# Filling the rotary attention's ring buffers inside layer 0, and running one batch's feed-forward inside the rotary attention's opening

## The chip, the cores and the metric

The kernel runs on one core of a Trainium2 chip. That core has five engines with a queue of instructions each, taken in order: TensorE (matrix products, PE in the profile; PEld is its weight loads), VectorE (DVE), ScalarE (ACT), GpSimd (POOL) and SyncE (SP, which here only issues DMAs). Products land in PSUM, everything else lies in SBUF; both are cut into 128 partitions. The metric is the device time of the whole program in microseconds (us), the median of several runs.

## The reference

Four layers of a network in float32, on 4 batches of 1024 tokens with 128 channels. Around the change it computes this:

```
x = x + 0.5 * _L0_ffn_ref(_layernorm(x), ...)      # experts, second time in layer 0
x = x + 0.5 * _L1_ffn_ref(_layernorm(x), ...)      # gated feed-forward
x = x + _L1_attn_ref(_layernorm(x), ...)           # rotary attention, 16 heads of 8
x = x + 0.5 * _L1_ffn_ref(_layernorm(x), ...)
...
def _L1_ffn_ref(x, w_gate, w_up, w_down):
    gate = x @ wg.T ; up = x @ wu.T                # 128 -> 384
    return (silu(gate) * up) @ wd.T
```

The rotary attention turns queries and keys by position, takes the softmax of their products over all 1024 keys, and weighs the values with it. Nothing in any of these steps crosses from one batch to another.

## The kernel before

The residual `X[b]` of each of the four batches stays in SBUF, channels in the partitions, tokens along the row (128x1024, two halves of 512).

**Layer 0** (`layer0`, `macaron`) is written as lanes of tasks. `lanes` interleaves them by costs written into their `yield`s; that gives the order of the program text. The order on each engine is then set at compile time by a list scheduler with a model of the hardware, which may issue an instruction of a later stage early when its operands and its memory are free. The lanes are: the expert blocks (`experts`: POOL gathers token rows by indirect DMA, L452, and scatters results, L478), the combines (`combine`: two `c_y` loads on SP, scaling, four transposes and one add into `X[b]` for each half, L503 to L513), and a lane with the routes, the layer's own attention (`middle0` to `middle3`, `l0_attn`) and then the feed-forward of each batch, `last(0)` to `last(3)` (`l1_ffn`, L604 to L637). `last(b)` waits for `combine1{b}`; `last(3)` takes PSUM banks from the pool `main`, the others from `side`. Attention and feed-forward hold their SBUF pools `l0a` and `l1f0` on the right side of the memory until layer 0 ends.

**The rotary attention** (`l1_attn`) has its TensorE order written by hand (`manual_schedule`): its own matrix products keep the order of the text, while those of other stages may still come in between. It first clears its rings on POOL (L663 to L669): four `qz`, four `kz`, four `va` (128x1024 each) and two `top`. Heads lie eight channels to a group of 32 partitions; row 0 of each group of `kz` is set to one, group by group, as `va`'s first column is. All of them lie in the pool `l1a`, which waits for the pools that held its memory before as a whole. Then `prepare(0)` normalizes batch 0 and makes dense queries, keys and values: a centering product (`cen`), variances (`var`), a broadcast of 1/std (`bc`), four projections, of which cosine and sine halves are multiplied on DVE (`rot1`, `rot2`) and added on POOL (`qd`, `kd`, L709), and a value product (`vp`). `spread(n)` copies a group of heads into a ring by eight small DMAs on SP and a POOL copy into `va`.

The main loop then takes 256 units. In each unit `greatest` finds row maxima (products of 32 rows, reduced on DVE, L736), and `scores` and `values` work 11 units (`LEAD`) behind it, so in the first 11 units only `greatest` runs. `prepare` of the next batch is spread over the units from the eleventh on. The products use PSUM pools of two double banks (`l1m`, tag `two`), three banks (`l1s`, tag `s`) and one (`l1o`).

```
            for z in (*qz, *kz, *va, *tops):
                nc.gpsimd.memset(z, 0.0)
            for z in va:
                nc.gpsimd.memset(z[:, :, :, 0:1], 1.0)
            for z in kz:
                for g in range(4):
                    nc.gpsimd.memset(z[32 * g : 32 * g + 1, :], 1.0)
```

Layer 2 then takes its SBUF pools from the right side again (`l2d`, `l1f1`, `l2a`).

Of the kernel before, what the change touches and what calls it, by code (L numbers as in the profile page):

```python
# [13 lines left out]
AF = mybir.ActivationFunctionType  # L14
ALU = mybir.AluOpType
AX = mybir.AxisListType

P = 128
# [3 lines left out]
NT = S // P  # L22
# [5 lines left out]
BLOCKS = blocks_of(GT)  # L28
MOE_W = 2 * FC * P + FC + D
HIDC = 3  # L30
LN_EPS = 1e-5
GN_EPS = 1e-5 * 64
L2_EPS = 1e-6
# [27 lines left out]
def _constants():  # L61

    p = np.arange(P)
    f = np.float32
    n8, n16 = np.arange(8), np.arange(16)
    t = np.arange(P)

    c0 = [
        ("ident", np.eye(P, dtype=f)),
        ("mean", np.full((P, P), 1.0 / P, f)),  # L70
        ("rev", np.broadcast_to((8 - n8).astype(f), (P, 8))),
        ("below", (p[:, None] < p[None, :]).astype(f)),
        ("ones", np.ones((P, P), f)),
        ("lane", np.broadcast_to(p.astype(f), (P, P))),
        ("column", np.broadcast_to(np.arange(BLOCKS, dtype=f), (P, BLOCKS))),
        ("full", np.broadcast_to((SLOTS * np.arange(GT)).astype(f), (P, GT))),
        ("center", np.eye(P, dtype=f) - f(1.0 / P)),
        ("place", 1.0 + p[:, None].astype(f)),
        ("tile", np.broadcast_to(np.arange(2 * GT, dtype=f), (P, 2 * GT))),
        *[  # L80
            (f"spare{g}", (1.0 + 2 * g * NT * P + p[:, None] + P * np.arange(blocks_of(g * NT))).astype(f))
            for g in range(1, GROUP + 1)
        ],
    ]

    dd = p % HD
    freqs = np.power(f(10000.0), -np.arange(0, HD, 2, dtype=f) / f(HD)).astype(f)
    angles = (np.arange(S, dtype=f)[:, None] * freqs).astype(f)
    sin, cos = np.sin(angles).astype(f), np.cos(angles).astype(f)
    sign = np.where(dd < HD // 2, -1.0, 1.0).astype(f)  # L90
    c1 = [
        ("cos", cos.T[dd // 2]),
        ("sin", sin.T[dd // 2] * sign[:, None]),
    ]

    n = np.maximum(t[None, :] - p[:, None], 0)
    bits = ((n[:, None, :] >> np.arange(7)[:, None]) & 1).astype(f)
    c2 = [("bit", bits), ("nobit", 1 - bits), ("causal", (t[None, :] >= p[:, None]).astype(f))]

    h, turned = p // HD, np.arange(2)[None, :, None]  # L100
    c3 = [
        ("sums", (h[:, None, None] == np.arange(32) - NH * turned).astype(f)),
        ("vrows", ((p % 32)[:, None, None] == NH * turned + h).astype(f)),
        ("bonus", (h[:, None] == p % NH).astype(f)),
        ("gcenter", np.eye(P, dtype=f) - (p[:, None] % NH == p % NH).astype(f) / HD),
        ("gmean", (p[:, None] % NH == n16).astype(f) / HD),
    ]
    return {"c0": c0, "c1": c1, "c2": c2, "c3": c3}
# [99 lines left out]
class Macaron:  # L208
# [433 lines left out]

    def l1_attn(self, m, c1):
        nc = self.nc
        scale = HD ** -0.5
        LEAD, RING = 11, 4
        v = nc.vector
        PE = mybir.EngineType.PE  # L650
        with ExitStack() as ctx:
            enter = ctx.enter_context
            wp = enter(self.tc.tile_pool(name="l1a", bufs=2))
            p1 = enter(self.psum("l1m", 2))
            p2 = enter(self.psum("l1s", 3))
            pa = enter(self.psum("l1o", 1))
            enter(self.tc.manual_schedule(engines={PE}))
            two = lambda shape=(P, S): self.t(p1, list(shape), "two")
            ring = lambda tag, shape, n: [self.t(wp, shape, f"{tag}{i}", bufs=1) for i in range(n)]
            qz, kz = ring("qz", [P, S], RING), ring("kz", [P, S], RING)  # L660
            va = ring("va", [P, NT, 4, 32], RING)
            tops = ring("top", [P, 4, 4, 32], 2)
            for z in (*qz, *kz, *va, *tops):  # L663
                nc.gpsimd.memset(z, 0.0)
            for z in va:
                nc.gpsimd.memset(z[:, :, :, 0:1], 1.0)
            for z in kz:
                for g in range(4):
                    nc.gpsimd.memset(z[32 * g : 32 * g + 1, :], 1.0)  # L669
            ons, dense = {}, {}  # L670

            def project(w, x):
# [134 lines left out]
                    v.scalar_tensor_tensor(X[:, c], y, m["bo"], X[:, c], ALU.add, ALU.add)  # L807
                    yield

            for _ in prepare(0):  # L810
                pass
            for n in range(RING):
                spread(n)
            units = B * 4 * 16
# [1 line left out]
            for k in range(units + LEAD + 1):  # L816
                first = k if k < units else None
                second = k - LEAD if 0 <= k - LEAD < units else None
                if k % 16 == LEAD + 1 and RING <= k // 16 + RING - 1 < 4 * B:
                    spread(k // 16 + RING - 1)  # L820
                if k % 64 == 10 and k // 64 + 1 < B:
                    running.append(prepare(k // 64 + 1))
                if first is not None and first % 8 == 0:
                    nms[first // 8] = self.t(wp, [P, 4, 2, 4], "nm", bufs=3)
                    qms[first // 8] = self.t(wp, [P, HALF], "qm", bufs=3)
                es = {}
                for pair in range(2):
                    if first is not None:
                        greatest(first, pair, nms[first // 8])
                    if second is not None:  # L830
                        scores(second, 1 - pair, qms[second // 8], es)
                    if pending:
                        at, then = pending
                        if at % 8 == 0 and pair == 0:
                            o = self.t(pa, [P, HALF], "o")
                        values(at, o, then, pair)
                if pending and at % 8 == 7:
                    running.append(normalized(at // 8, o))
                pending = (second, es) if second is not None else None
                if first is not None and first % 8 == 7:  # L840
                    running.append(shifted(first // 8, nms[first // 8], qms[first // 8]))
                running = [r for r in running if next(r, self) is not self]
            while running:
                running = [r for r in running if next(r, self) is not self]

# [402 lines left out]

    def layer0(self, moe, m, right, enter, ffn):
        m["wqkvc"] = self.centered(m["wqkv"], 3 * D)  # L1250
        pa, pf = enter(right, "l0a"), enter(right, "l1f0")
        side, main = self.side, self.main

        def more(route):
            attn = lambda b, *after: (f"middle{b}", after, lambda: self.l0_attn(side, pa, m, b))
            last = lambda b, ps: (f"last{b}", (f"combine1{b}",), ffn(pf, ps, b))
            return (
                [
                    route(0, (0,), ps=main), route(0, (1,)), route(0, (2, 3)),
                    *[attn(b, f"combine0{b}") for b in range(B)],  # L1260
                    last(0, side), last(1, side), last(2, side), last(3, main),
                ],
                [route(1, (0, 1), "middle0", "middle1", "combine03"), route(1, (2,), "middle2"), route(1, (3,), "middle3")],
            )


        groups = [(0,), (1,), (2, 3)], [(0, 1), (2,), (3,)]
        marks = {(0, (0,)): "_1", (0, (1,)): "_2", (0, (2, 3)): "_0", (1, (0, 1)): "_0", (1, (2,)): "_1", (1, (3,)): "_2"}
        self.macaron("l0", moe, AF.Gelu, groups, marks, more)
# [29 lines left out]

    def run(self, stages):  # L1300
        nc = self.nc
        self.X = []
        self.c0 = self.load("c0")
        for b in range(B):
            X = self.t(self.res, [P, S], f"x{b}")
# [20 lines left out]
        for n, name in enumerate(stages):  # L1326
# [3 lines left out]
            if name in ("l0", "l2"):  # L1330
                with self.psum("main", 4) as self.main, self.psum("side", 4) as self.side, sb(name + "moe") as self.fp:
# [2 lines left out]
                    nc.vector.tensor_copy(moe["both"][:, 0:P], self.c0["center"])  # L1334
                    nc.scalar.copy(moe["both"][:, P:], self.centered(moe["rw"], NE))
                    with ExitStack() as right:
                        enter = lambda stack, name, bufs=2: stack.enter_context(sb(name, bufs, side="right"))
                        m = dict(weights(name + "a"))
                        ffn = lambda wp, ps, b: lambda: self.l1_ffn(ps, wp, weights("l1f"), b)
                        if name == "l2":  # L1340
                            self.c2 = weights("c2")
                        if name == "l0":
                            self.layer0(moe, m, right, enter, ffn)
                        else:
                            self.layer2(moe, m, right, enter, ffn)
            elif name == "l1_attn":
                with sb("ln1") as self.lnp:
                    self.l1_attn(weights("l1a"), weights("c1"))
            else:
                f, t, c3 = self.l3_ffn_weights(weights("l3f")), self.l3_time_weights(weights("l3a")), weights("c3")  # L1350
                self.layer3(f, t, c3)
        for b in range(B):
            nc.sync.dma_start(out=self.out[:, b * S : (b + 1) * S], in_=self.X[b])

# [35 lines left out]
```

## Time and profile before

| what | us |
|---|---|
| median of 3 runs | 3132.94 (3131.44 to 3135.03) |
| the profiled execution's own time | 3239.76 |
| span of its trace, first to last instruction | 3237.5 |
| TensorE busy in the span | 2766.3 (85%) |
| VectorE busy | 1834.3 (57%) |
| ScalarE busy | 1626.5 (50%) |
| GpSimd busy | 799.3 (25%) |
| layer 0's last expert product ends | 887.0 |
| last batch's feed-forward, first to last product | 897.8 to 928.1 |
| first product of `greatest` | 965.8 |
| first product of `scores` | 1008.6 |
| last product of `values` | 2024.4 |

Durations are taken from the one profiled execution, which took 107 us longer than the median of the undisturbed runs. In the lists below, a line gives start, duration, engine, source line, operation, output and inputs by the program's names with their shapes, how many instructions are merged into the line, and in brackets how long the engine stood idle before it and what released it. `PEclk` is the share of TensorE's full clock that was granted.

### The profile page before, as it was taken

The page shows a single profiled execution, that of the slowest core. Times are in us where ns is not written, and L with a number is a line of the kernel's source. Part 1 is how long each engine was busy: PE and PEld are TensorE (multiplying, and loading weights), DVE is VectorE, ACT ScalarE, POOL GpSimd, SP SyncE. Part 2 cuts the span into 40 slices and gives each one's busy share as a digit, 9 for nine tenths or more (in the row PEclk, how much of TensorE's full clock was granted, in tenths as well). Part 3 has the DMA queues.
Part 4 walks back from the last instruction along what each step waited for, and adds up shares of the span by engine and source line. Part 5 has one row for each costly group of instructions (what it writes and reads, how often), then busy time and mean ns, then how long its engine had stood idle before and what let it go on. Part 6 is the DMA issues. An engine that isn't in the chain of part 4 may idle for free. (4 is left out here: it accounts for less than half of the span.)

```text
span 3237.5 us, 47507 instructions
## 1 busy us (share of the span) xinstructions
PE 2766.3 (85%) x17694; PEld 1584.7 (49%) x17694; DVE 1834.3 (57%) x3214; ACT 1626.5 (50%) x3631; POOL 799.3 (25%) x748
## 2 busy tenths in 40 slices
PE   5877537778969999999999999987988976899997
PEld 4666415665633333333333333567877865334333
DVE  3476986774226676676677673452565622354764
ACT  3555524657712565566465666444453544345342
POOL 3566306552440000000000000046434463010110
PEclk8889758889977999999999999989998988788997
DMA  6656415563500000000000000057665675000000
GB/s 211 208 169 196 125 50 160 159 188 119 154 19 9 5 6 4 6 5 6 20 6 4 3 1 1 21 166 233 198 186 163 209 228 162 0 1 1 7 7 13
DMA packets 122886, 277.57 MB, mean 86 GB/s; under 512 B 18016, under 2 KB 67296, under 8 KB 122528
## 3 DMA queue, kind: packets, MB, share of 16 engines
q1 hardware_dynamic: 101792, 231.77, 23.7%
q0 software_dynamic: 20864, 42.77, 4.5%
q8 instruction: 140, 2.29, 0.3%
q14 instruction: 90, 0.74, 0.1%
HBM read 238.43 MB, written 31.85 MB: 83 GB/s over the span
## 5 line engine op out<-in xcount | busy, mean ns | idle before, releaser
L736 DVE TENSOR_REDUCE nm<-two 128x2 f32<-128x1024 f32 x512 | 626.6, 1224 | 290.8 <-PE s L229 271.4
L759 ACT ACTIVATE e<-s 128x512 f32<-128x512 f32 x1024 | 555.8, 595 | 408.7 <-PE s L229 405.7
L466 ACT ACTIVATE e_h<-bank,e_w 128x128 f32<-128x128 f32 x1304 | 451.0, 367 | 495.3 <-PE bank L229 382.9
L229 PE MATMUL bank<-e_x,e_w 128*128 128x128 f32 x2608 | 543.6, 312 | 127.9 <-ACT e_h L466 65.7
L229 PE MATMUL s<-qm,kz 32*128 32x512 f32 x2048 | 635.7, 645 | 0.8 <-ACT e L759 0.8
L229 PE MATMUL two<-kz,qz 32*128 32x512 f32 x2048 | 595.0, 666 | 21.4 <-POOL va L724 2.5
L452 POOL DMA_INDIRECT e_xg<-rows,g_source x326 | 331.6, 1017 | 822.1 <-DVE g_target L419 356.1
L229 PE MATMUL bank<-e_w,e_h 128*128 128x128 f32 x2608 | 475.5, 298 | 56.7 <-ACT e_h L466 31.3
L229 PEld LDWEIGHTS bank<-e_x,e_w 128*128 128x128 f32 x2608 | 413.4, 205 | 219.9 <-ACT e_h L466 113.1
L478 POOL DMA_INDIRECT res<-e_y,g_target x326 | 368.6, 1131 | 300.1 <-DVE e_y L477 135.4
L229 PEld LDWEIGHTS bank<-e_w,e_h 128*128 128x128 f32 x2608 | 387.6, 206 | 89.8 <-ACT e_h L466 46.6
L229 PE MATMUL o<-e,va 128*32 128x256 f32 x4096 | 329.2, 393 | 0.1
L229 PEld LDWEIGHTS two<-kz,qz 32*128 32x128 f32 x2048 | 160.1, 189 | 240.5 <-issue 163.3
L229 PEld LDWEIGHTS o<-e,va 128*32 128x32 f32 x4096 | 81.0, 108 | 391.8 <-issue 371.8
L458 DVE COPY e_x<-bank 128x128 f32<-128x128 f32 x326 | 92.7, 285 | 263.7 <-PE bank L456 139.7
L477 DVE TENSOR_TENSOR e_y<-bank,e_w 128x128 f32<-128x128 f32 x326 | 93.6, 287 | 213.9 <-PE bank L229 191.0
L229 PEld LDWEIGHTS s<-qm,kz 32*128 32x128 f32 x2048 | 207.0, 184 | 10.9 <-issue 7.8
L724 POOL COPY va<-vd 128x256 f32<-128x256 f32 x16 | 6.7, 431 | 626.2 <-PE o L229 537.9
L1131 POOL TENSOR_TENSOR z<-st,r 128x512 f32<-128x512 f32 x32 | 46.2, 1444 | 417.5 <-DVE st L1124 240.2
L456 PE MATMUL bank<-c,e_xg 128*128 128x128 f32 x326 | 97.0, 300 | 39.7 <-DMA e_xg<-rows,g_source 36.2
L466 ACT ACT_TABLE_LOAD x53 | 68.0, 1283 | 24.0 <-PE bank L229 18.0
L544 DVE TENSOR_TENSOR prod<-qkv 128x2048 f32<-128x2048 f32 x32 | 73.1, 2286 | 5.5 <-ACT qkv L536 5.5
(304 smaller groups left out, 3489.0 us busy)
## 6 DMA issues: line engine op xcount, KB each, us to landing
e_w<-in_l0m_dram SPq DMA_DIRECT2D x170, 578.0 KB
e_w<-in_l2m_dram SPq DMA_DIRECT2D x156, 578.0 KB
c_y<-res SPq DMA_DIRECT2D x32, 512.0 KB
rows<-g_xt SPq DMA_DIRECT2D x16, 512.0 KB
e_xg<-rows,g_source POOLq DMA_INDIRECT x326
res<-e_y,g_target POOLq DMA_INDIRECT x326
x<-in_x_dram SPq DMA_DIRECT2D x4, 512.0 KB
qz<-qd SPq DMA_DIRECT2D x64, 32.0 KB
```

The lines of the kernel that those rows point to most:

```text
L229: self.nc.tensor.matmul(out, lhsT, rhs, start=start, stop=stop)
L452: nc.gpsimd.indirect_dma_start(out=xg, out_offset=None, in_=rows[:, :], in_offset=at(source[:, k : k + 1]))
L456: nc.tensor.transpose(tp, xg, self.c0["ident"])
L458: nc.vector.tensor_copy(x, tp)
L466: nc.scalar.activation(h[:, fc, :], o[:, fc, :], func, bias=w[:, 2 * FC * P + fc : 2 * FC * P + fc + 1])
L477: nc.vector.tensor_tensor(y, o, w[:, MOE_W - D :], ALU.add)
L478: ins = nc.gpsimd.indirect_dma_start(out=res[:, :], out_offset=at(target[:, k : k + 1]), in_=y, in_offset=None)
L544: v.tensor_tensor(pr, q.unsqueeze(2).to_broadcast(sh), k.unsqueeze(1).to_broadcast(sh), ALU.mult)
L724: nc.gpsimd.tensor_copy(va[n % RING][:, :, :, 1 : 1 + HD], dense[b, "vd"][:, :, 32 * g4 : 32 * g4 + 32].rearrange("p t (h d) -> p t h d", ...
L736: v.tensor_reduce(nm[:, it, h, 2 * pair : 2 * pair + 2], s, AX.X, ALU.max, negate=True)
L759: nc.scalar.activation(es[g], s, AF.Exp, scale=scale)
L1131: (pool if i else v).tensor_tensor(z, st[:, 0:HALF], r, ALU.mult)
```

## The change

Rings: `qz`, `kz` and `top` move to a new pool `l1rings` on the right side, filled by a new function `l1_rings`. The four one-row fills of each `kz` and its clearing become one POOL copy of a new constant column `first` (1 in partitions 0, 32, 64, 96), broadcast along the row. In layer 0 a task `swap`, behind `middle3` in its lane, closes the attention's pool `l0a` and calls `l1_rings` there; the feed-forward's pool `l1f0` goes to the left side. `va` stays in `l1a` and is cleared behind `prepare(0)` in the text. `l1a` waits for single tiles in place of whole pools (`reuse_waits="tile"`).

Feed-forward: `last(3)` leaves layer 0. A generator `feed(b, hf)` does the same work for one half of that batch, in eight steps. `prepare(0)` advances the first half by one step after each of its yields from the third on, which takes it to its end; the second half advances by one step at the end of each unit, from unit 1 to unit 8. It uses the PSUM tag `s` and the SBUF tag `e` of the attention.

```diff
+    def l1_rings(self, pool):
+        fill = self.nc.gpsimd
+        for tag, n, shape in (("qz", RING, [P, S]), ("kz", RING, [P, S]), ("top", 2, [P, 4, 4, 32])):
+            self.ring[tag] = [self.t(pool, shape, f"{tag}{i}") for i in range(n)]
+        for z in (*self.ring["qz"], *self.ring["top"]):
+            fill.memset(z, 0.0)
+        for z in self.ring["kz"]:
+            fill.tensor_copy(z, self.c0["first"].to_broadcast([P, S]))
...
-            wp = enter(self.tc.tile_pool(name="l1a", bufs=2))
+            wp = enter(self.tc.tile_pool(name="l1a", bufs=2, reuse_waits="tile"))
...
-            for z in (*qz, *kz, *va, *tops):
-                nc.gpsimd.memset(z, 0.0)
-            for z in va:
-                nc.gpsimd.memset(z[:, :, :, 0:1], 1.0)
-            for z in kz:
-                for g in range(4):
-                    nc.gpsimd.memset(z[32 * g : 32 * g + 1, :], 1.0)
+            qz, kz, tops = (self.ring[tag] for tag in ("qz", "kz", "top"))
+            va = [self.t(wp, [P, NT, 4, 32], f"va{i}", bufs=1) for i in range(RING)]
...
-            for _ in prepare(0):
-                pass
+            def feed(b, hf):
+                c = slice(hf * HALF, (hf + 1) * HALF)
+                bank, one = lambda: self.t(p2, [P, HALF], "s"), lambda: self.t(wp, [P, HALF], "e", bufs=10)
+                cen, sq, xc = bank(), one(), one()
+                self.mm(cen, self.c0["center"], self.X[b][:, c])
+                nc.scalar.activation(sq, cen, AF.Square)
+                v.tensor_copy(xc, cen)
+                yield
+                var = bank()[:, 0:4]
+                for i in range(4):
+                    self.mm(var[:, i : i + 1], sq[:, i * P : (i + 1) * P], self.c0["mean"][:, 0:1])
+                std, r = self.t(self.lnp, [P, 4], "fstd"), self.t(self.lnp, [P, 4], "frstd")
+                nc.scalar.activation(std, var, AF.Sqrt, bias=self.eps_ln)
+                v.reciprocal(r, std)
+                yield
+                bc, xn, hs = bank(), one(), []
+                for i in range(4):
+                    self.mm(bc[:, i * P : (i + 1) * P], r[:, i : i + 1].to_broadcast([P, P]), self.c0["ident"])
+                v.tensor_tensor(xn, xc, bc, ALU.mult)
+                yield
+                for i in range(HIDC):
+                    g, u, s = bank(), bank(), one()
+                    self.mm(g, f["wg"][:, i, :], xn)
+                    nc.scalar.activation(s, g, AF.Silu)
+                    self.mm(u, f["wu"][:, i, :], xn)
+                    hs.append(one())
+                    v.tensor_tensor(hs[i], s, u, ALU.mult)
+                    yield
+                yield
+                o = bank()
+                for i in range(HIDC):
+                    self.mm(o, f["wd"][:, i, :], hs[i], start=i == 0, stop=i == HIDC - 1)
+                self.add_half(b, c, o)
+
+            late = [feed(b, hf) for b in self.late for hf in range(2)]
+            for n, _ in enumerate(prepare(0)):
+                if late and n >= 2:
+                    next(late[0], None)
+            for z in va:
+                nc.gpsimd.memset(z, 0.0)
+                nc.gpsimd.memset(z[:, :, :, 0:1], 1.0)
...
                 running = [r for r in running if next(r, self) is not self]
+                if late and next(late[0], self) is self:
+                    late.pop(0)
...
-        pa, pf = enter(right, "l0a"), enter(right, "l1f0")
+        early = right.enter_context(ExitStack())
+        pa, pf = enter(early, "l0a"), enter(right, "l1f0", side="left")
+        self.late = [B - 1]
+        def swap():
+            early.close()
+            self.l1_rings(enter(self.rings, "l1rings", 1))
+            yield 0
...
-                    last(0, side), last(1, side), last(2, side), last(3, main),
+                    ("swap", (), swap), *[last(b, side) for b in range(B) if b not in self.late],
```

After the rotary attention the ring pool is closed.

More of the change, by code (lines that the diff above doesn't have):

```diff
@@ L30 @@
 HIDC = 3
+RING = 4
 LN_EPS = 1e-5
@@ L77, in _constants @@
         ("center", np.eye(P, dtype=f) - f(1.0 / P)),
+        ("first", (p[:, None] % 32 == 0).astype(f)),
         ("place", 1.0 + p[:, None].astype(f)),
@@ L638, in l1_ffn, with l1_attn @@
             yield 3
-    def l1_attn(self, m, c1):
+    def l1_rings(self, pool):
[6 more added lines that the diff above has]
+            fill.tensor_copy(z, self.c0["first"].to_broadcast([P, S]))
+    def l1_attn(self, m, c1, f):
         nc = self.nc
         scale = HD ** -0.5
-        LEAD, RING = 11, 4
+        LEAD = 11
         v = nc.vector
@@ L658, in l1_attn @@
             two = lambda shape=(P, S): self.t(p1, list(shape), "two")
[L659 to L662, printed above, removed]
-            for z in (*qz, *kz, *va, *tops):
-                nc.gpsimd.memset(z, 0.0)
-            for z in va:
-                nc.gpsimd.memset(z[:, :, :, 0:1], 1.0)
-            for z in kz:
-                for g in range(4):
-                    nc.gpsimd.memset(z[32 * g : 32 * g + 1, :], 1.0)
+            qz, kz, tops = (self.ring[tag] for tag in ("qz", "kz", "top"))
+            va = [self.t(wp, [P, NT, 4, 32], f"va{i}", bufs=1) for i in range(RING)]
             ons, dense = {}, {}
@@ L1301, in run @@
         nc = self.nc
-        self.X = []
+        self.X, self.ring, self.rings, self.late = [], {}, ExitStack(), []
         self.c0 = self.load("c0")
@@ L1336, in run @@
                     with ExitStack() as right:
-                        enter = lambda stack, name, bufs=2: stack.enter_context(sb(name, bufs, side="right"))
+                        enter = lambda stack, name, bufs=2, side="right": stack.enter_context(sb(name, bufs, side=side))
                         m = dict(weights(name + "a"))
@@ L1347, in run @@
                 with sb("ln1") as self.lnp:
-                    self.l1_attn(weights("l1a"), weights("c1"))
+                    if not self.ring:
+                        self.l1_rings(self.rings.enter_context(sb("l1rings", 1, side="right")))
+                    self.l1_attn(weights("l1a"), weights("c1"), weights("l1f") if self.late else None)
+                    self.rings.close()
             else:
@@ L1351, in run @@
                 self.layer3(f, t, c3)
+        self.rings.close()
         for b in range(B):
```

## The prediction

> **What bounds it now.** I read the page's slices first: DMA falls to nothing and TensorE dips between layer 0 and the attention. Then the timeline there, then windows for the clock. The chain of waits covers only the last 500 us, so this place is read from the timeline. These are its lines at the end of layer 0.
>
> ```profile
> 887.59 0.97 POOL L478 DMA_INDIRECT res<-e_y,g_target  x1 [0.47 <-DVE e_y L477]
> 889.84 1.01 SPq L503 DMA_DIRECT2D c_y<-res  x2
> 895.67 2.05 PE L512 MATMUL bank<-c,c_y 128*128 128x128 f32 x7 [8.69 <-DVE c_y L509]
> 897.11 0.68 DVE L251 SCALAR_TENSOR_TENSOR x<-bank,x 128x512 f32<-128x512 f32 x1
> 897.84 2.03 PE L229 MATMUL bank<-x,c 128*128 128x512 f32 x2
> ...
> 927.91 1.88 PE L229 MATMUL two<-x,c 128*128 128x512 f32 x4
> ...
> 928.14 3.62 POOL L664 MEMSET qz<- 128x1024 f32 x4 [39.58 <-PE bank L229]
> ...
> 940.02 15.72 POOL L669 MEMSET kz<- 1x1024 f32 x16
> ...
> 955.84 2.33 POOL L709 TENSOR_TENSOR qd<-rot,rot 128x1024 f32<-128x1024 f32 x1
> ...
> 958.21 1.22 DVE L704 TENSOR_TENSOR rot<-attn_c,two 128x1024 f32<-128x1024 f32 x1 [14.50 <-POOL qd L709]
> ```
>
> Three serial pieces follow each other. (1) From 887 to 895.7 TensorE waits for the last combine's loads. (2) The last batch's feed-forward stands alone from 897.8 to 928.1, a chain of small steps. (3) The ring fill starts when that ends, takes 27.7 us, and the add `qd`, whose operands were complete at 943.7 (second `rot`, 942.48 + 1.22), waits behind it until 955.84: 12.1 us lost. Then come the units, and their clock:
>
> ```profile
> core 0: us, PE busy (x) PEld busy (x) DVE busy (x) ACT busy (x) POOL busy (x), PEclk, DMA share, GB/s
> 897.70:928.10 30.40, 27.25 (x75) 14.36 (x75) 8.72 (x15) 7.61 (x11) 0.00 (x0) 0.80 0.00 1
> 928.10:965.80 37.70, 18.18 (x68) 12.10 (x68) 6.91 (x7) 4.49 (x5) 33.08 (x40) 0.76 0.04 6
> 965.80:1008.60 42.80, 41.63 (x96) 13.80 (x96) 27.51 (x24) 0.00 (x0) 0.09 (x1) 0.50 0.14 20
> ```
>
> In the last row, the 11 units before `scores`, TensorE is busy throughout at half clock and DVE only 64%: 3.40 us a unit (two reductions of 1.22 with 0.86 of waiting).
>
> **Where the sum starts.** All of it is the time of the first `scores` product, 1008.6 now; behind it both kernels do the same. I read full-clock costs as starts of successive products: a 512-wide matrix product (two instructions) 0.86 us, at half clock 1.71 (907.4 against 921.0).
>
> **Part 1, the early start of `prepare(0)`.** Today it cannot start before `last(3)` leaves the banks of `main`, which `two` takes over. Without `last(3)` their last reader is the final expert's DVE add, ending 887.31. `X[0]` has been complete since 779.6 (its second feed-forward add). The profile shows that stages interleave as memory frees: layer 2's first products (`bank<-x,c`, 2026.18) run between the attention's own transposes (2025.06 and 2027.14). So the centering product and the variances should fall into the hole from 887.3 to 895.7: four instructions, 2 to 3.4 us, the two ACT passes 2.0, the variances 2.0, std and reciprocal 0.6 with waits: done near 895. Gain if so: the place of these steps; if not, they start behind the transposes at 900.0.
>
> **Part 2, first half of the feed-forward inside `prepare(0)`.** It needs the first half of `X[3]`, added at 897.8. TensorE work from there at full clock: `cen` 0.86, variances 1.0, broadcast 1.05, three pairs of gate and up 5.2, down 2.6: 10.7 us. Of `prepare(0)`: broadcast 2.1, four projections 6.9, values 2.1: 11.1 us. Together 21.8. The clock is cold after the hole, as it is today up to 913; that adds some 4.5. Walking through in text order, with a DVE or ACT step (0.69, 0.60) and about 0.2 for each hand-over, I get: `feed` variances end 902.5, broadcasts 908.7, first gate and up 913.3, `wq` 915.0, `wqt` 918.5, second `rot` 920.0, `qd` 922.4, key `rot`s 925.1, `kd` 927.5. Today the first `greatest` comes 2.8 us behind `kd` (962.99 to 965.8, the key DMAs), so it comes at 930.3, 35.5 us earlier than now. With the start at 900.0 the same walk gives 935.5. ACT gains two table loads of 1.28; they lie beside products.
>
> **Part 3, POOL.** 12 clearings and 16 one-row fills leave the path. `va`'s (four of 0.953, four of 0.156: 4.4 us) remain; their memory is free from 890 on, POOL is idle then, and `va` is not needed until unit 12: nothing. At worst they stand ahead of `kd`: +4.4. SP issues the same 32 DMAs of `spread`; no queue is longer.
>
> **Part 4, the fill inside layer 0.** Four memsets of 0.95, two of 0.53, and four broadcast copies of 128x1024. No such copy is in the trace; the nearest rows are L724 (128x256 in 0.43, so 1.7) below and the two-input add (2.33) above. Nothing excludes a cost of a memset, 0.95; I take 1.7: 11.7 us in all. It can start when the attention leaves `l0a`: L588's last add ends at 734.4, and right behind it (734.77) DVE runs layer 2's `gp`, whose memory is that side's. From 735 to 783 POOL is busy 7.7 us of 48, with holes of 9 to 11 us; the fill fits, price nothing. Without that cover it stands before the ten gathers at 783.4 to 795, which TensorE waits for: +11.7. I take +1. [...]
>
> **Part 5, second half of the feed-forward in units 1 to 8.** Before the clock, DVE: 11 units of 2.45 are 27.0, plus seven feed steps, 4.3. TensorE at full clock: 1.75 a unit plus the feed's 10.7. In a gate-and-up unit DVE's product waits for the second of the two products (0.6 behind the last reduction): 3.75 a unit. In step 8 the down products (2.6) outlast the reduction by 1.5: 4.6. Sum: 2.5 + 3 x 3.2 + 3 x 3.75 + 2.5 + 4.6 + 2.5 + 4.4 (unit 10 with the next batch's centering) = 37.3 us against 42.8: a gain of 5.5. At half clock a unit is 3.4 of TensorE alone, eleven are 37.4; the feed adds 20.3 and the centering 3.8: 61.5, a loss of 18.7. These are the two ends.
>
> [...]
>
> ```profile
> 970.00:975.00 5.00, 4.99 (x14) 1.58 (x14) 3.28 (x3) 0.00 (x0) 0.00 (x0) 0.50 0.36 52
> 990.00:995.00 5.00, 5.00 (x14) 1.79 (x16) 3.86 (x4) 0.00 (x0) 0.00 (x0) 0.50 0.00 0
> 1005.00:1010.00 5.00, 4.88 (x12) 1.51 (x12) 1.06 (x2) 1.22 (x2) 0.00 (x0) 0.61 0.00 0
> 1010.00:1015.00 5.00, 3.46 (x24) 1.36 (x24) 2.68 (x3) 4.43 (x7) 0.00 (x0) 1.00 0.00 0
> ```
>
> Being busy with 32-row products does not release it; 3.8 us of the 128-row centering at 1004.9 did. The change puts 128-row products into eight of these units, and the units now follow warm products instead of the idle stretch from 946 to 959. I take warm (37.3), at about two in three.
>
> **Part 6, layer 2.** `l2d` now overlays the rings and waits for their last readers (up to 2021.6, the last scores). Its G operations (about 6 us of DVE) ran at 1582; at worst they run at 2022 to 2028, beside idle DVE time but ahead of a few normalizing steps: 0 to 6, I take 2.
>
> **Sum.** First `scores` at 930.3 + 37.3 = 967.6, 41.0 earlier; less 3 for waits my walk does not see (some 15 hand-overs of 0.2), less 1 and 2 from parts 4 and 6: 35 us. The execution of 3239.76 becomes 3204.8. This stretch has no bulk DMA and runs alone, so I take the same 35 us off the median: 3132.94 - 35 = 3098. (Scaled by 3132.94/3239.76 it would be 34.)
>
> **Rivals.**
> *Late start* (0.17): the scheduler puts `prepare(0)` behind the transposes: first `greatest` at 935.5, gain 30, 3103. For it: text order; against it: the interleaving at 2026.
> *Cold units* (0.24): the mixed units don't hold the clock. Gain 35 - 24.2 = 11: 3122. For it: the 0.50 rows; against it: 1004.9.
> *Blocked gathers* (0.09), the slower end: POOL is in order, and the fill waits for `l0a`. If the compile-time model thinks the attention done earlier than it is, fill and wait stand in front of gathers and scatters. Price: wait plus 11.7 less about 19 (six gathered tiles ahead at 3.2 us a block). It decides from a wait of some 42 us on, a fill queued before about 692; at 680 (54 us) it costs 47 against the gain of 35: 3145. For it: every POOL issue of 690 to 734 sits within 4 us of its neighbour; against it: that the model would have to err by 42 us.
> *Nothing moves* (0.05): what is saved at 930 is given back, because the units were waiting for something else, SP's 21 us of DMA issues say: 3133. Against it: units wait only for TensorE and DVE in the trace.
>
> **Chances and range.** Forecast 0.45, its own range 3089 to 3107 with the late start. A measurement tells about 0.2%, 6.3 us, from no change. Faster: 0.45 + 0.17 + 0.24, less 0.02 of the cold case's upper end: 0.84; same 0.07; slower 0.09. The range runs from 3086 (41 plus the unspent 6 us of allowances) to 3126 (cold units with half of the POOL price), leaving out the blocked gathers and what is left of no movement.
>
> **What would show it.** Right: no product of `l1f_wg` between 890 and the first `two`; ring fills between 735 and 783; `two<-x,c` near 888; first `greatest` near 930; PEclk near 1.0 in the units; `scores` near 970. Wrong: PEclk 0.50 in the units, gaps at `e_xg` around 735, or `qd` again behind POOL work.

## The result, and the profile after

The changed kernel takes 3094.52 us (3091.85 to 3101.51, 6 runs) against 3132.1 (3123.61 to 3135.03, 6 runs) for the kernel before, run beside it: a ratio of 0.9893, 95% interval 0.9881 to 0.9905, which is a gain of 30 to 37 us. The medians are 37.6 us apart. The forecast was 3098.

The profiled execution of the kernel before was a slow one (3239.76 us), as were those of the experiments a to h, so times are compared only with the kernel before run beside them, and traces by stretches:

| stretch (us) | before | before again (a) | changed | changed again (i) | d |
|---|---|---|---|---|---|
| start to the last expert's add | 887.3 | 891.3 | 838.0 | 839.9 | 895.0 |
| from there to the first product of `greatest` | 78.5 | 78.5 | 43.6 | 43.4 | 44.0 |
| from there to the first of `scores` | 42.8 | 42.8 | 44.3 | 44.2 | 45.1 |
| from there to the start of the last of `values` | 1015.4 | 1015.5 | 1010.2 | 1010.2 | 1011.1 |
| from there to the end | 1213.5 | 1216.9 | 1155.9 | 1155.9 | 1217.3 |

Experiment d does the same work as the changed kernel, in an execution whose trace is 120.4 us longer. Of these, 118.3 lie in the two outer rows, where the bulk transfers are, and 0.4 to 0.9 in each of the middle ones. So the middle rows carry the comparison. Between before and changed, 34.9 us are gained up to `greatest`, 1.5 lost in the units and 5.2 gained behind, together 38.6. Between a and d, whose runs stand beside the same runs of the kernel before, it is 34.5 gained, 2.2 lost and 4.4 gained, together 36.6. The gain in the traces is thus known to about 2 us, and it agrees with the medians.

The windows of the changed kernel over the first two stretches, to be set beside the three of before (columns: window, its length, busy us and instructions of PE, PEld, DVE, ACT, POOL, then granted clock, DMA share, GB/s):

```profile
837.70:881.60 43.90, 32.65 (x112) 20.53 (x113) 14.29 (x24) 10.74 (x19) 10.58 (x15) 0.81 0.13 32
881.60:925.90 44.30, 40.90 (x136) 14.70 (x136) 30.99 (x31) 5.22 (x7) 0.65 (x2) 0.81 0.13 19
```

Feed-forward and preparation now share one window in which TensorE works 32.65 of 43.9 us, and POOL's share fell from 33 us in the stretch to 10.6. In the units the mean clock rose from 0.50 to 0.81, yet they take as long: the feed's products filled what the clock gave.

The timeline of the changed kernel at layer 0's end (weight loads left out):

```profile
837.73 0.29 DVE L479 TENSOR_TENSOR e_y<-bank,e_w 128x128 f32<-128x128 f32 x1 [1.15 <-PE bank L231]
838.07 1.98 PE L231 MATMUL two<-x,c 128*128 128x512 f32 x4 [0.38 <-DVE e_y L479]
...
844.37 2.44 ACT L510 ACTIVATE c_y<-c_y,g_p 128x128 f32<-128x128 f32 x8 [7.22 <-DMA c_y<-res]
...
846.72 1.00 ACT L686 ACTIVATE sq<-two 128x1024 f32<-128x1024 f32 x1
846.75 2.05 PE L514 MATMUL bank<-c,c_y 128*128 128x128 f32 x7 [6.69 <-DVE c_y L511]
...
849.45 3.41 PE L231 MATMUL two<-c,sq 128*128 128x1 f32 x16
```

The centering product starts as the last expert's bank comes free. But its square on ScalarE stands behind the combine's scaling, which waits for the loads, and the variances stand behind the transposes on TensorE.

### The profile page after: what moved, and what is told of

It is laid out like the page before. It is cut to its first block, busy times and chain, and to the rows that moved or that the text cites. A ratio compares the mean times of both kernels' runs of the same rounds, so it can differ in the third digit from the quotient of the medians.

```text
span 3092.0 us, 47511 instructions
## 1 busy us (share of the span) xinstructions
PE 2709.1 (88%) x17694; PEld 1564.1 (51%) x17694; DVE 1834.9 (59%) x3215; ACT 1623.9 (53%) x3633; POOL 780.5 (25%) x732
## 5 line engine op out<-in xcount | busy, mean ns | idle before, releaser
L231 PE MATMUL bank<-e_x,e_w 128*128 128x128 f32 x2608 | 535.5, 309 | 87.1 <-ACT e_h L468 54.7
L231 PE MATMUL two<-kz,qz 32*128 32x512 f32 x2048 | 578.0, 647 | 21.0 <-DVE nm L740 4.6
L231 PE MATMUL bank<-e_w,e_h 128*128 128x128 f32 x2608 | 463.3, 293 | 27.1 <-ACT e_h L468 17.2
L231 PEld LDWEIGHTS bank<-e_w,e_h 128*128 128x128 f32 x2608 | 379.3, 202 | 50.6 <-ACT e_h L468 30.7
L231 PEld LDWEIGHTS two<-kz,qz 32*128 32x128 f32 x2048 | 153.8, 184 | 228.9 <-issue 162.7
L231 PEld LDWEIGHTS s<-qm,kz 32*128 32x128 f32 x2048 | 206.9, 183 | 11.3 <-issue 7.7
```

Of the source, the lines that this page charges most:

```text
L231: self.nc.tensor.matmul(out, lhsT, rhs, start=start, stop=stop)
```

## Experiments

Every comparison of time is with the kernel before run beside it. Stretches are the three middle rows of the table; where two numbers are given, they are those up to `greatest` and the units from there to `scores`.

**a, the kernel before again.** No edit.

> The kernel before, unchanged, for a second profile of it. Both theories: the stretch from the last expert's add to the first product of scores takes the same 121 to 122 us as in the first profile. If the 107 us by which the first profiled execution was longer than the median lie in the stages with bulk transfers (layers 0 and 2), this profile is shorter there and the same between. Rival: the excess is spread evenly, then the stretch is some 118 us here.

Its stretches are in the table: from the last expert's add to `scores` 121.3 us, as in the first trace. But this execution was as long as the first (a span of 3244.9 us against 3237.5), so it could not show where the excess over the median lies. The rival of an evenly spread excess falls by d instead: spread evenly, some 43 of its 120.4 us would be in the middle rows, and 2.1 are.

**b, rings alone.**

```diff
-        self.late = [B - 1]
+        self.late = []
...
-                    ("swap", (), swap), *[last(b, side) for b in range(B) if b not in self.late],
+                    ("swap", (), swap), last(0, side), last(1, side), last(2, side), last(3, main),
```

> The rings are filled in layer 0, the last batch's feed-forward stays where it was in the kernel before. Theory of three pieces: only the 12.1 us that the key and query adds waited behind the fill are saved, first product of greatest 12 to 14 us earlier, units cold as before: 3132 - 13 = 3119 us. Rival, that the fill was the main cost: 3132 - 25 = 3107 us or less.

Ratio 0.9948 (0.9930 to 0.9965). The stretch to `greatest` is 66.8 us, 11.7 less than before; the units take 43.0. The fill was worth its wait of 12.1 us and no more.

**c, feed-forward alone.** The lines L657 to L669 of before are back in `l1_attn` in place of the ring pool, and `l1a` waits for whole pools.

> The last batch's feed-forward moves into the rotary attention, the rings are filled as in the kernel before. Theory of three pieces: the fill starts some 12.7 us after the last expert's add and ends 40 us after it, the query add then, first product of greatest some 50 us after that add (79 before, 43.9 in the changed kernel): 3132 - 28 = 3104 us. Rival, that the fill was the main cost: 3120 to 3125 us.

Ratio 0.9914 (0.9895 to 0.9933). Stretches 48.8 and 45.0. The fill now runs from 906.7, 11.3 us behind the last expert's add, beside the feed-forward's first half:

```profile
906.70 3.62 POOL L677 MEMSET qz<- 128x1024 f32 x4 [10.05 <-PE bank L514]
...
927.65 1.22 DVE L720 TENSOR_TENSOR rot<-attn_c,two 128x1024 f32<-128x1024 f32 x1 [0.96 <-PE two L231]
...
934.40 2.33 POOL L722 TENSOR_TENSOR qd<-rot,rot 128x1024 f32<-128x1024 f32 x1
```

The add `qd` has its operands at 928.87 and waits 5.5 us for the fill. In the changed kernel the stretch is 43.6: taking the fill out of the way is worth only 5.2 us there, since the feed-forward hides the rest. So the parts overlap: 11.7 + 29.7 = 41.4 us singly, 34.9 together.

**d, the fill's call at the head of the attention.**

```diff
             early.close()
-            self.l1_rings(enter(self.rings, "l1rings", 1))
             yield 0
```

(Where layer 0 has not filled the rings, the changed kernel's own code fills them at the head of the attention.)

> As the changed kernel, but the call that fills the rings stands at the head of the rotary attention's text and not in layer 0's lane. If the early place in the text is what matters: the fill runs behind layer 0's end on POOL, 9 us, still before the query add, so 3094 to 3098 us. Rival: single-tile waits alone let the scheduler issue the fill when the attention's tiles leave; then the fill sits near 690 us as in the changed kernel and the time is 3094 us.

Ratio 0.9888 (0.9868 to 0.9908), stretches 44.0 and 45.1: the changed kernel's within a microsecond. Its POOL timeline:

```profile
738.27 0.97 POOL L480 DMA_INDIRECT res<-e_y,g_target  x1 [2.75 <-DVE e_y L479]
739.25 1.86 POOL L653 MEMSET qz<- 128x1024 f32 x2
741.44 0.98 POOL L480 DMA_INDIRECT res<-e_y,g_target  x1 [0.33 <-DVE e_x L460]
742.41 1.85 POOL L653 MEMSET qz<- 128x1024 f32 x2
```

Even from the head of the attention's text the fill is issued right behind layer 0's own attention, between the scatters. The place in the text does not matter here. What lets the fill go early is that the rings lie in a pool of their own, in `l0a`'s memory and with single-tile waits; in c they lay in `l1a`, which waited for whole pools. Which of these counts was not tried apart.

**e, the double banks elsewhere.**

```diff
-            p1 = enter(self.psum("l1m", 2))
             p2 = enter(self.psum("l1s", 3))
             pa = enter(self.psum("l1o", 1))
+            p1 = enter(self.psum("l1m", 2))
```

> The attention's PSUM pools are opened in another order, so that the double banks lie where layer 0's last combine transposes and not where its experts were. Theory: the first centering product then comes behind the transposes, 12 us after the last expert's add and not at once, and the first product of greatest 4 to 5 us later than in the changed kernel (48 us after that add; 43.6 there). Time 35 - 5 = 30 us under the kernel before. Rival, that the early start is worth nothing because ScalarE stands behind the combine's loads anyway: unchanged, 43.6.

46.9 us to `greatest`, 3.3 more than the changed kernel; ratio 0.9911 (0.9890 to 0.9932). The centering product now starts behind the transposes, at 913.20, 11.3 us behind the last expert's add (901.86). The early start is worth 3 us: not the 4 to 5 forecast, but not nothing.

**f, the last combine's scaling on GpSimd.**

```diff
+            if lone:
+                at = slice(4 * h, 4 * h + 4)
+                nc.gpsimd.tensor_tensor(
+                    y[0][:, at, :], y[0][:, at, :], plan["p1"][:, at, :].to_broadcast([P, 4, P]), ALU.mult
+                )
             for j in range(4):
                 i = 4 * h + j
-                nc.scalar.mul(y[0][:, i, :], y[0][:, i, :], plan["p1"][:, n * NT + i, :])
+                if not lone:
+                    nc.scalar.mul(y[0][:, i, :], y[0][:, i, :], plan["p1"][:, n * NT + i, :])
```

(`lone` is true for the group of the last batch alone.)

> The last combine's scaling by the first weight moves from ScalarE to GpSimd (two products of 128x512). Theory: ScalarE's square of batch 0 then follows its centering product at once, some 2.5 us after the last expert's add and not 8.7; the variances are done before the transposes, and the first product of greatest comes 3 to 4 us earlier, 40 us after that add. Time 38 us under the kernel before. Rival: the feed-forward's first step waits for the combine anyway and the whole is bound there: unchanged.

No gain: 44.3 and 45.7, ratio 0.9892 (0.9869 to 0.9915). Its timeline says why:

```profile
906.60 1.02 ACT L693 ACTIVATE sq<-two 128x1024 f32<-128x1024 f32 x1 [2.94 <-PE two L231]
...
913.41 2.05 PE L521 MATMUL bank<-c,c_y 128*128 128x128 f32 x7 [6.85 <-DVE c_y L518]
...
916.11 3.42 PE L231 MATMUL two<-c,sq 128*128 128x1 f32 x16
```

ScalarE is freed: the square comes 2.1 us behind the last expert's add (904.52). TensorE then idles 6.85 us with the variances' operand ready from 907.6 on, because in its queue the transposes stand first. The theory named the right wait and missed the one behind it.

**g, the second half of the feed-forward alone, ahead of the units.**

```diff
+            for _ in late.pop() if late else ():
+                pass
+            late.clear()
```

> The second half of the late feed-forward runs alone between the preparation of batch 0 and the units, not inside the units. Theory, that the units hide it at half of its price: the units without it take 42 to 43 us at half clock as in the kernel before (or 30 at full clock if they stay warm), the half alone some 18: the first product of scores comes 6 to 17 us later than in the changed kernel. Time 18 to 29 us under the kernel before. Rival, that the feed steps cost the units all they take: within 2 us of the changed kernel.

56.1 and 41.3 us: 9.5 slower over both than the changed kernel; ratio 0.9908 (0.9885 to 0.9930). Alone the half costs 12.5 us, inside the units 3.0 (4.0 to 4.5 against the units of e and f, 45.2 and 45.7). And the units without it, from 956.9 on, run at a clock of 0.50 within two windows although they follow dense work at 1.00:

```profile
951.90:956.90 5.00, 5.00 (x12) 1.82 (x10) 1.37 (x2) 1.06 (x2) 0.00 (x0) 1.00 0.34 50
956.90:961.90 5.00, 3.66 (x19) 1.11 (x18) 4.27 (x4) 0.00 (x0) 0.00 (x0) 0.87 0.28 42
961.90:966.90 5.00, 5.00 (x14) 1.45 (x12) 3.38 (x3) 0.00 (x0) 0.00 (x0) 0.50 0.01 3
...
986.90:991.90 5.00, 4.00 (x13) 1.59 (x13) 3.42 (x4) 0.00 (x0) 0.00 (x0) 0.50 0.00 0
```

**h, unread products of 128 rows in seven of the first eleven units.**

```diff
+                if k in (0, 1, 2, 3, 7, 9, 10):
+                    self.mm(self.t(p2, [P, HALF], "s"), self.c0["center"], self.X[0][:, 0:HALF])
```

> Seven units of the first eleven get one more product of 128 rows and 512 columns whose result nobody reads. Theory of the clock: 128-row products hold the granted clock; the units then run near 1.0 from the second on and take 38 to 40 us with 6 us more of products in them (44.3 in the changed kernel). Time 39 us under the kernel before. Rival, that the units are slow from the work itself: 44.3 plus 5 to 8, 29 us under the kernel before.

The units take 41.1 us with 6 us more of products in them, 3.2 less than the changed kernel. The windows of h, five microseconds each from its first `greatest`, and then those of the changed kernel:

```profile
949.10:954.10 5.00, 4.97 (x14) 1.71 (x14) 2.45 (x2) 0.00 (x0) 0.68 (x2) 0.80 0.35 52
954.10:959.10 5.00, 5.00 (x21) 1.75 (x20) 3.17 (x4) 1.88 (x2) 0.00 (x0) 0.86 0.31 47
959.10:964.10 5.00, 5.00 (x30) 2.69 (x28) 3.82 (x5) 1.55 (x2) 0.00 (x0) 1.00 0.36 52
964.10:969.10 5.00, 5.00 (x22) 1.73 (x21) 4.44 (x6) 0.60 (x1) 0.00 (x0) 1.00 0.15 24
```

```profile
881.60:886.60 5.00, 4.99 (x14) 1.96 (x16) 2.57 (x3) 0.00 (x0) 0.65 (x2) 0.82 0.34 50
886.60:891.60 5.00, 5.00 (x14) 1.02 (x10) 3.02 (x3) 1.54 (x2) 0.00 (x0) 0.50 0.31 47
891.60:896.60 5.00, 4.66 (x24) 2.47 (x21) 4.45 (x5) 1.88 (x3) 0.00 (x0) 0.84 0.35 52
896.60:901.60 5.00, 5.00 (x17) 2.24 (x17) 2.90 (x4) 0.00 (x0) 0.00 (x0) 0.50 0.15 24
901.60:906.60 5.00, 5.00 (x21) 1.92 (x21) 4.00 (x5) 1.19 (x2) 0.00 (x0) 0.97 0.00 0
906.60:911.60 5.00, 3.79 (x18) 0.99 (x12) 4.43 (x6) 0.60 (x1) 0.00 (x0) 1.00 0.00 0
```

In the first four windows TensorE is nearly always busy in both; what it multiplies differs. In the fifth and sixth of the changed kernel it works on the feed's gate and up products, and the clock is back, though TensorE is busy for only 3.79 of 5 us. The clock theory had the right sign: 3.2 of the 4 to 6 us forecast came, and the full clock was held from the third window on. In whole time h's ratio is 0.9887 (0.9863 to 0.9911), not to be told from the changed kernel's.

**i, j, k: the changed kernel again, unread products in the hole behind the first centering product, and these together with h's.**

```diff
+                if b == 0:
+                    spare = two()
+                    for i in range(8):
+                        h = i % 2
+                        self.mm(spare[:, h * HALF : (h + 1) * HALF], c["center"], X[:, h * HALF : (h + 1) * HALF])
```

> The changed kernel once more, beside the two that follow. Both theories: 43.6 us from the last expert's add to the first product of greatest, 44 to 45 to the first of scores, 35 to 38 us under the kernel before.

> As the changed kernel, with eight products of 128 rows and 512 columns that nobody reads behind batch 0's centering product, in the 6.7 us in which TensorE waits for the last combine's loads. Theory of the clock: the steps from the variances to the second broadcast (3.41, 2.06, 1.87, 3.76 us in the changed kernel's trace) then run at full clock, some 5 us less: first product of greatest at 39 us behind the last expert's add. Rival, that dependencies and not products set this stretch: 43 us or, where the extra products delay the transposes, 44.

> The extra products of the hole and those of the seven units together. Theory of the clock: both gains add, 39 us to the first product of greatest and 41 from there to the first of scores, some 8 us under the changed kernel. Rival: the units gain only as much as they lost to a cold start, and the sum is 4 us or less.

| kernel | to `greatest` | to `scores` | median us | ratio to before (95%) |
|---|---|---|---|---|
| i, changed | 43.4 | 44.2 | 3094.48 | 0.9888 (0.9872 to 0.9905) |
| j, hole | 40.9 | 45.0 | 3091.68 | 0.9888 (0.9871 to 0.9904) |
| k, hole and units | 40.9 | 42.2 | 3089.11 | 0.9875 (0.9857 to 0.9893) |

In j the eight products keep TensorE busy in the hole. The variances then take 1.85 us in place of 3.41 and the feed's centering 1.10 in place of 2.06. Then the clock falls again and the first broadcast takes 3.76 as before:

```profile
838.80:843.80 5.00, 4.95 (x12) 2.32 (x13) 0.00 (x0) 0.00 (x0) 4.73 (x8) 1.00 0.29 83
843.80:848.80 5.00, 4.14 (x12) 1.66 (x11) 1.51 (x6) 3.45 (x10) 0.20 (x2) 1.00 0.52 155
848.80:853.80 5.00, 4.25 (x29) 3.16 (x27) 2.65 (x7) 2.94 (x4) 0.00 (x0) 0.98 0.01 3
853.80:858.80 5.00, 5.00 (x24) 5.00 (x25) 0.59 (x3) 1.55 (x2) 0.00 (x0) 0.50 0.00 0
```

So 2.5 of the 5 us came, and the units gave 0.8 of them back. Both fillings together save 4.5 us over the two stretches (87.6 against 83.1): more than the rival's 4, and well short of the 8 forecast. k's median is the lowest of the study, but its interval overlaps i's.

## Why the prediction was right, and where not

**Part 1, the early start.** Right in its mechanism (838.07, at the instant the bank came free), wrong in "done near 895" for the variances: that is 7.7 us behind the last expert's add, and they ended at 14.8. The walk put ScalarE's passes directly behind the product and the variances ahead of the transposes; both engines' queues had the combine first (after's timeline, f). e prices the early start at 3.3 us, not 5.2.

**Part 2, the feed-forward beside `prepare(0)`.** Right. Counted from the last expert's add, the walk gave 35.1 for the end of `qd`, 40.2 for `kd` and 43.0 for `greatest`; the trace has 35.8, 40.9 and 43.6. The late variances were made good because the clock came up some 3 us sooner than the walk assumed: it was 0.50 from 844.0 to 860.9 and 1.00 from there to the units, 23 us behind that add, where the walk had 913, 26 behind. That these two errors cancel was luck.

**Part 3, POOL.** Right: `va` is cleared at 839.2 to 843.2, in an idle stretch, and `qd` starts 0.1 us behind its second operand.

**Part 4, the fill in layer 0.** Right at nothing, and no run shows the 1 us that was allowed for it. The copies were over-priced: 1.03 us each, not 1.7, 9.1 us in all.

```profile
694.76 3.98 POOL L655 COPY kz<-c 128x1024 f32<-128x1024 f32 x4
```

The four DVE steps beside these copies took about as long as elsewhere: two copies `e_x` 0.29 and 0.24 us, a product `e_y` 0.29 and a reciprocal `frstd` 0.19, against medians of 0.28, 0.29 and 0.20 over the whole trace.

**Part 5, the units.** This is the step that failed: "I take warm (37.3)". Measured 44.3, between the two ends, so a loss of 1.5 in place of a gain of 5.5. The warm case rested above all on one place in before: behind 3.78 us of 128-row centering (1004.91) the clock went from 0.50 to 0.91 (1008.7 to 1010) and 1.00. The mixed units did not hold the clock. It was full at the last product before the units and fell to 0.50 within 4 us of 32-row products; it came back to 0.99 from 891.6 to 895.0, behind the feed's centering, and for longer only from 901.9 to 922.4 (1.00), with the gate and up products. A mean of 0.81 over 44.3 us says that some 17 us ran at half clock, so that TensorE needed up to 8 us more for the same products (an estimate from that mean); 7.0 were lost. g shows the same fall in units without any feed (0.50 from 961.9 to 996.9), and in h, with 128-row products in most units, the clock was 1.00 from the third window on. The cold-units rival (61.5) overshot as well: with the feed in them, the units had a clock of 1.00 for 20.5 us of their second half.

**Part 6 and behind.** The allowance of 2 us for layer 2's G operations had the wrong sign. They now run from 1928.7 on, in DVE's idle time at the attention's tail. At their old place, 1582 in before, they sat among the units: before and c, which have them there, take 35.9 and 37.4 us between two outputs of the attention (the 17th and the next one) where the changed kernel and b take 33.9. That is 2.0 of the 5.2 us gained behind `scores`. The other 3.2 lie at three places of about 1.1 us where the mean clock is 0.96 to 1.00 over 45 us in the changed kernel and 0.92 to 0.96 in before. Whether they belong to the change is not shown: h, whose work there is the changed kernel's, takes 134.8 us over the three, the changed kernel 132.3 and before 135.7. What makes the clock dip more or less there was not tried. "Behind it both kernels do the same" was wrong by these 5.2 us.

**The sum.** 34.9 - 1.5 + 5.2 = 38.6 against 41.0 less allowances of 6: the total came close by luck, because the failed 7 us of the units were balanced by the unspent allowances and by the 5.2 behind, which nobody had in the sum. The range's lower end of 3086 counts the allowances twice, since 41.0 is the gain before they are taken off; 41 gives 3092, and the result lies inside either way. Of the rivals, late start did not happen (e shows what it would have cost), blocked gathers did not, and nothing of the gain was given back.

## What to carry to other kernels

A stage that stands alone between two others is worth moving beside its neighbour when each is a chain of short steps: the same half of the feed-forward cost 12.5 us alone and 3.0 to 4.5 inside work bound elsewhere. Gains of parts that hide each other don't add (41.4 us singly, 34.9 together): price each with the other in place. And when an early start is counted, read the order of every engine's queue at that spot: in f, freeing ScalarE only showed TensorE's queue behind it, 6.85 us idle.

## What was not expected of the hardware

A POOL clearing of one partition took as long as one of all 128: 0.943 us for 1x1024 (L669) and 0.953 for 128x1024 (L664). The 16 one-row fills were thus 15.7 of the fill's 27.7 us, and four broadcast copies of 1.03 us replace them together with the clearing.

In these traces TensorE's clock did not follow how busy the profile calls the engine, but what ran in it. Products of 32 rows kept PE busy 4.99 to 5.00 of 5 us at a clock of 0.50 for 25 us and more (before from 965.8, g from 961.9). In j, one-column variances and narrow broadcasts kept it busy 5.00 of 5 us (853.8 to 858.8), also at 0.50. With products of 128 rows and 512 columns the clock held 1.00, alone (j, in the hole, 838.8 to 848.8) or among those of 32 rows (h, from its third window on), in the changed kernel even where PE was busy for only 3.79 of 5 us (906.6 to 911.6). Whether the rows or the columns count was not tried apart.
